# A graph attention layer: each node tile projected directly behind the transposes of its second block

## The chip, the core and the metric

The kernel runs on one core of a Trainium2 chip, in one launch. A core has five engines that work side by side, each through its own instructions in order: PE (TensorE, matrix products into PSUM), DVE (VectorE), ACT (ScalarE), POOL (GpSimd, which here issues the gathers) and SP (SyncE, which here issues loads and stores). They meet through semaphores. The metric is the device time of the whole launch in microseconds (us).

## The reference

The input x has 4096 rows of 512 values, all float32; adj is a 4096 x 4096 matrix in which under one entry in a hundred is above zero. Two layers follow each other, each on a layer norm with a relu, each added to x:

```python
# layer 0
h = relu(layernorm(x))
d = rowsum(adj) ** -0.5
x = x + relu((d[:, None] * adj * d[None, :]) @ h @ W0 + b0)
# layer 1
h = relu(layernorm(x))
hw = h @ W1
e = leaky_relu(hw @ a[:512] + (hw @ a[512:]).T, 0.2)      # 4096 x 4096
p = softmax(where(adj > 0,  e, -1e12), axis=1)
q = softmax(where(adj > 0, -e, -1e12), axis=1)
x = x + elu(concat([p @ h, -(q @ h)], axis=1) @ wtrans)   # wtrans: 1024 x 512
```

## The kernel before

Layer 0 is a dense product over adj, in groups of node tiles (a tile is 128 nodes). It also writes what layer 1 needs: for each node a row of a table in HBM (its h, its score, and its bits of the adjacency), and for each pair of blocks a list of the neighbours. Layer 1 uses that few entries of adj are above zero.

In layer 1 a **block** is 64 nodes, and a **pair** is two blocks, so one node tile. There are 32 pairs. The first of them (`PAIR0`, 16) is worked on at the end of layer 0, so that its transposed result `ut0` lies ready; the other 31 are worked on by `sparse_layer1`, whose list `order` holds their 62 blocks, two of a pair behind each other. Below, the even block of a pair is the first, the odd one the second.

For each pair GpSimd issues 22 indirect DMAs (`gather`, L487), each of which fetches 128 table rows of 644 words into SBUF. They go into three buffers: `g0` (8 gathers), `g1` (6) and `g2` (8). The even block of the pair uses `g0` and `g1`, the odd one `g1` and `g2`. Each of these buffers exists twice (`g_pools[k % 2, a]`), so that a pair shares its buffers with the pair two before it: a gather into one has to wait until that pair's last reader of it is done.

The work on one block r has these steps:

- `weights(r)`: for both of its buffers DVE adds the scores (z, L501), ACT and DVE make the leaky relu (L1633, L1634), ACT takes two exponentials (p, L513), for the two softmaxes, and DVE multiplies with the mask (L523). DVE then sums p (total, L1639).
- `product(r)`: PE sums total over the partitions (cs, L554), DVE makes the reciprocal (rl, L556 and L557); PE multiplies p with the gathered rows in 22 products (u, L530), and ACT scales the result into SBUF (us, L1667).
- `turn(r)`: PE transposes us in four parts (tp, L564), and ACT copies them into one half of the pair's tile `ut` in two copies (L569), one for each softmax.
- `finish1(n)`, once for a pair: SP loads the rows of x1 (L1677); PE multiplies `ut` with wtrans in eight products (o, L1681), four for each softmax; DVE and ACT make the elu and the addition (L1689 to L1693), and SP stores the tile (L1694).

The profile counts each float32 matmul as two, so a product of a block shows as 44 rows.

In `sparse_layer1` nobody writes the order of the engines by hand. The program is written down in the order of the loop over k (L1723 to L1744), and a scheduler builds each engine's order from it before the kernel runs; only some instructions (the gathers among them) are kept in program order. At step k the loop writes the product of block k, the gathers of a later pair, the weights of block k + 2, the transposes of block k - 1, and, at each odd k from 3 on, the projection of the pair that holds block k - 3. PAIR0 is projected at k = 2. Behind the loop come the last transposes and the last projection. Some other steps stand in the same loop: `copy_rows` (SP copies table rows to further tables), `load_s` (SP loads the score rows of coming blocks), and at k = 40 `judge`, a test whether the lists were long enough.

In the built program PE's order around one pair is, before the change: u of the even block; tp of the odd block of the pair before; u of the odd block; tp of the even block; o of the pair before; and so on with the next pair. ACT's order is: the exponentials of the next pair's even block; us of the even block; the two `ut` copies of the odd block of the pair before; the exponentials of the next pair's odd block; us of the odd block; the `ut` copies of the even block.

Of the kernel before, what the change touches and what calls it, by code (L numbers as in the profile page):

```python
# [269 lines left out]
def gcn_gat_kernel(  # L270
# [55 lines left out]
    def bank(name):  # L326
        return ps.tile([P, 512], F32, tag="ps", name=name)
# [4 lines left out]
    with sbuf(name="init", bufs=1) as init:  # L332
        column = init.tile([P, P], F32, name="column")
        nc.vector.memset(column[:, 0:1], 0.0)
        n = 1
# [140 lines left out]
    def copy_rows(queue, g, j, n):  # L476

        r = j // EJ * ER + j % EJ * P
        return queue.dma_start(
            out=table[g][r : r + n * P, :ROW_W], in_=table[tab0][r : r + n * P, :ROW_W]  # L480
        )
# [78 lines left out]
    def turn_u(r, u, ut):  # L560

        tp = ps.tile([P, FC, 2, 2, SB], F32, tag="ps", name=f"tp{r}")
        for c in range(FC):
            nc.tensor.transpose(  # L564
                tp[:, c].rearrange("p h g i -> p (h g i)"), u[:, c * P : (c + 1) * P], ident
            )
        for g in range(2):
            half = ut[:, g, :, (r % 2) * RB : (r % 2 + 1) * RB]
            nc.scalar.copy(half.rearrange("p c (h i) -> p c h i", h=2), tp[:, :, :, g, :])  # L569
# [4 lines left out]
    with sbuf(name="y0", bufs=1) as y_pool, sbuf(name="wa", bufs=1) as wa_pool, sbuf(name="bits", bufs=4) as bits_pool, sbuf(name="small0", bufs=4) as small, ExitStack() as rest, ExitStack() as lists:  # L574
# [473 lines left out]
        i0, n = GROUPS[0]  # L1048
        with sbuf(name="w0", bufs=1) as w0_pool, sbuf(name="ain", bufs=9) as ain, sbuf(name="xs", bufs=5) as x_pool, sbuf(name="at6", bufs=5) as at_pool, sbuf(name="bits6", bufs=3) as bits6, sbuf(name="ln", bufs=3) as ln_pool, sbuf(name="marks", bufs=6) as mark_pool:
# [32 lines left out]
            order = {engine.PE, engine.DVE, engine.Activation, engine.SP}  # L1082
            with tc.manual_schedule(engines=order):
# [37 lines left out]
                for j in range(NJ):  # L1121
                    q, turn = 4 * j + 5, j + 3 < NJ
# [443 lines left out]
    def sparse_layer1():  # L1566
        nonlocal verdict
        with ExitStack() as pools:
# [34 lines left out]
            gath, wgt, us, uts, srow = {}, {}, {}, {PAIR0: ut0}, {}  # L1603

            def load_s(k):

                srow[k] = s_pool.tile([P, 4 * P], F32, tag="s", name=f"s{k}")
                return nc.sync.dma_start(
                    out=srow[k], in_=s_dram[4 * k * P : 4 * (k + 1) * P].partition_broadcast(P)
                )  # L1610

            def gather1(n, a):
                k = pairs.index(n)
                gt = g_pools[k % 2, a].tile([P, CHUNKS[a], ROW], I32, tag="g", name=f"g{a}_{n}")
                gather(gt, n, a, True)
                gath.setdefault(n, []).append(gt)
# [6 lines left out]
            def weights(r):  # L1623

                nk = sum(CHUNKS[r % 2 : r % 2 + 2])
                p = p_pool.tile([P, nk, 2, 2, SB], F32, tag="p", name=f"p{r}")
                s = srow[r // 8][:, r % 8 * RB : (r % 8 + 1) * RB]

                for gt, k, n in parts(r):
                    z = bank(f"z{r}_{k}")[:, : n * RB].rearrange("p (k c) -> p k c", c=RB)  # L1630
                    scores(s, z, gt[:, :, ROW_T : ROW_T + 1].bitcast(F32))
                    y = tmp.tile([P, n, RB], F32, tag=f"y{n}", name=f"y{r}_{k}")
                    nc.scalar.activation(y, z, AF.Copy, scale=ALPHA)  # L1633
                    nc.vector.tensor_tensor(z, z, y, ALU.max)  # L1634
                    exps(z, p[:, k : k + n], leaky=False, pin=r in first)
                    mask_out(r, p[:, k : k + n], gt[:, :, ROW_W:].bitcast(U8))
                total = small.tile([P, 2 * RB], F32, tag="total", name=f"total{r}", bufs=3)
                q = p.rearrange("p k h g i -> p (h g i) k")
                nc.vector.tensor_reduce(total, q, AX.X, ALU.add)  # L1639
                for k in range(n_late if r in with_late else 0):  # L1640
                    q = lates[r][:, k].rearrange("p h g i -> p (h g i)")
                    nc.vector.tensor_tensor(total, total, q, ALU.add)
                wgt[r] = (p, total)
# [7 lines left out]
            def product(r):  # L1651
                p, total = wgt.pop(r)

                rl = None if r in first else inverse_sums(small, r, total)
                u = bank(f"u{r}")

                def row(k):
                    gt, k0, n = parts(r)[k >= parts(r)[1][1]]
                    return gt[:, k - k0, :F].bitcast(F32)

                half_products(r, u, p, row, HALVES[r % 2], r not in with_late)
                if r in with_late:
                    ks = range(n_late)
                    half_products(r, u, lates.pop(r), lambda k: late_h[:, k, :F], (ks, ks), begin=False)
                rl = rl or inverse_sums(small, r, total)
                us[r] = work.tile([P, F], F32, tag="us", name=f"us{r}")
                nc.scalar.activation(us[r], u, AF.Copy, scale=rl)  # L1667

            def turn(r):
                if r % 2 == 0:  # L1670
                    uts[r // 2] = ut_pool.tile([P, 2, FC, P], F32, tag="ut", name=f"ut{r // 2}")
                turn_u(r, us.pop(r), uts[r // 2])

            def finish1(j):
                ut = uts.pop(j)
                x1 = work.tile([P, F], F32, tag="x1", name=f"x1_{j}")
                nc.sync.dma_start(out=x1, in_=x1_dram[j])  # L1677
                po = bank(f"o1_{j}")
                for g in range(2):
                    for c in range(FC):  # L1680
                        nc.tensor.matmul(  # L1681
                            po,
                            ut[:, g, c, :],
                            wts[g][:, c, :],
                            start=g == 0 and c == 0,
                            stop=g == 1 and c == FC - 1,
                        )
                e = work.tile([P, F], F32, tag="eo", name=f"eo{j}", bufs=1)
                nc.vector.tensor_scalar(e, po, 0.0, None, ALU.min)  # L1689
                nc.scalar.activation(e, e, AF.Exp)  # L1690
                y = work.tile([P, F], F32, tag="y", name=f"y1_{j}", bufs=1)
                nc.vector.scalar_tensor_tensor(y, po, 0.0, x1, ALU.max, ALU.add)
                nc.vector.scalar_tensor_tensor(e, e, -1.0, y, ALU.add, ALU.add)  # L1693
                nc.sync.dma_start(out=out[j * P : (j + 1) * P, :], in_=e)  # L1694
# [7 lines left out]
            order = [r for n in pairs for r in (2 * n, 2 * n + 1)]  # L1702
# [20 lines left out]
            for k, r in enumerate(order):  # L1723
                product(r)
                if k % 6 == 1 and k // 6 < len(later):
                    for j, n in GROUPS[-2:]:
                        tc.keep_in_program_order(copy_rows(nc.sync, later[k // 6], j, n))
                if k + 4 - k % 2 < len(order):
                    for a in ((0,), (1, 2))[k % 2]:
                        gather1(order[k + 4 - k % 2] // 2, a)  # L1730
                if k + 2 < len(order):
                    weights(order[k + 2])
                    if wanted and order[k + 2] % 8 == 7:
                        load_s(wanted.pop(0))
                if k:
                    turn(order[k - 1])
                if k == 2:
                    finish1(PAIR0)
                if k == 40:
                    verdict = judge(small)  # L1740
                if k % 2 and k > 1:
                    finish1(order[k - 3] // 2)
            turn(order[-1])
            finish1(order[-1] // 2)  # L1744

    sparse_layer1()
    bad = nc.values_load(
        verdict[0:1, 0:1],
# [38 lines left out]
```

## Time and profile before

| what | us |
|---|---|
| median of 3 runs (lowest, highest) | 2099.77 (2090.87, 2101.19) |
| the profiled execution | 1951.6 |
| its span, first to last instruction | 1949.7 |
| granted TensorE clock, mean share of full speed | 0.984 |
| start of the products of `sparse_layer1` | 1053.7 |
| first issue of the last gather | 1899.0 |
| o of the last tile starts | 1934.2 |

The profile shows one execution. For each engine it gives when it was busy; a matmul's end is modelled, so PE's busy time is an upper reading. A row of an instruction group is: source line, engine, operation, what it writes and reads (buffer numbers left out), count, then busy time in us with the mean of one in ns, and the time that the engine sat idle just before, with what ended that. A row of the timeline is: start, duration, engine, line, operation and, in brackets, the idle time before it and what released it. A row of the waits is: who waited for what, us in total, times, and the longest. In the rows of DMA issues the last number is the median time in us from issue to landing.

The same stage in windows of time (from the span's start; busy time of each engine, with the number of instructions, the granted clock, the share of time that the DMA engines were busy, and GB/s):

```profile
1200.00:1400.00 200.00, 199.61 (x852) 76.59 (x849) 123.63 (x177) 61.48 (x133) 153.09 (x155) 1.00 0.89 292
1400.00:1600.00 200.00, 191.69 (x802) 73.72 (x800) 122.18 (x174) 60.85 (x132) 153.39 (x154) 0.99 0.89 289
1600.00:1800.00 200.00, 192.68 (x816) 73.94 (x814) 122.88 (x176) 60.90 (x133) 153.17 (x154) 1.00 0.87 274
```

The five busy columns are PE's matmuls, PE's weight loads, DVE, ACT and POOL.

### The profile page before, as it was taken

The page shows a single profiled execution, that of the slowest core. Times are in us where ns is not written, and L with a number is a line of the kernel's source. Part 1 is how long each engine was busy: PE and PEld are TensorE (multiplying, and loading weights), DVE is VectorE, ACT ScalarE, POOL GpSimd, SP SyncE. Part 2 cuts the span into 40 slices and gives each one's busy share as a digit, 9 for nine tenths or more (in the row PEclk, how much of TensorE's full clock was granted, in tenths as well). Part 3 has the DMA queues.
Part 4 walks back from the last instruction along what each step waited for, and adds up shares of the span by engine and source line. Part 5 has one row for each costly group of instructions (what it writes and reads, how often), then busy time and mean ns, then how long its engine had stood idle before and what let it go on. Part 6 is the DMA issues. An engine that isn't in the chain of part 4 may idle for free.

```text
span 1949.7 us, 23088 instructions
## 1 busy us (share of the span) xinstructions
PE 1858.9 (95%) x7752; PEld 1038.0 (53%) x7752; DVE 1317.1 (68%) x2879; ACT 636.2 (33%) x1185; POOL 902.6 (46%) x978
## 2 busy tenths in 40 slices
PE   7999989999999999999597999999999999999998
PEld 3444438888888888888332333333333333333333
DVE  5666659747897999896446766566566656656653
ACT  5777752112122212121122333233233223323321
POOL 2101001001232322232367777777777777777770
PEclk9999999999999999999798999999999999999999
DMA  9999955778467575867579898989889888888880
GB/s 350 371 336 335 332 199 193 241 223 282 132 198 238 170 256 169 265 208 235 156 242 345 259 316 278 311 270 312 291 292 301 274 281 265 282 277 261 275 277 31
DMA packets 185206, 503.47 MB, mean 258 GB/s; under 512 B 29107, under 2 KB 37971, under 8 KB 185078
## 3 DMA queue, kind: packets, MB, share of 16 engines
q0 software_dynamic: 70128, 265.46, 42.4%
q1 hardware_dynamic: 108832, 225.80, 34.1%
q10 hardware_dynamic: 6118, 10.64, 1.5%
q8 instruction: 63, 1.03, 0.2%
q14 instruction: 65, 0.53, 0.1%
HBM read 457.44 MB, written 103.02 MB: 287 GB/s over the span
## 4 chain that ended last, share of the span: by engine, by line
PE 63%; POOL 11%; DMA 10%; issue 9%; DVE 5%; ACT 1%; SPq 0%; DVEq 0%; POOLq 0%; ACTq 0%
PE p L1020 24%; PE u L530 15%; POOL g L487 11%; PE o L1681 7%; PE yp L809 6%; PE acc L979 5%; DMA g<-table,idx 4%; DMA ld<-li,off 3%; PE q L1354 2%; DMA at<-in_adj_t 1%; PE tp L564 1%; PE counts L794 1%; PE tx L758 1%; DVE p L523 1%; DMA xt<-in_x 1%
## 5 line engine op out<-in xcount | busy, mean ns | idle before, releaser
L487 POOL DMA_INDIRECT g<-table,idx x704 | 702.9, 998 | 224.4 <-issue 197.7
L530 PE MATMUL u<-g,p 128*64 128x512 f32 x2728 | 600.5, 596 | 4.2 <-DVE p L523 4.2
L530 PEld LDWEIGHTS u<-g,p 128*64 128x64 f32 x2728 | 190.8, 137 | 361.4 <-issue 333.2
L501 DVE TENSOR_TENSOR z<-g,s 128x512 f32<-128x512 f32 (+1 forms) x124 | 78.2, 631 | 283.2 <-DMA g<-table,idx 232.7
L1020 PE MATMUL p<-y,at 128*128 128x256 f32 x832 | 249.8, 382 | 5.7 <-DVE w L893 4.8
L1020 PE MATMUL p<-t,sums 128*128 128x256 f32 x832 | 246.4, 381 | 7.3 <-DVE t L994 7.3
L1020 PE MATMUL p<-y,sums 128*128 128x256 f32 x832 | 248.6, 380 | 0.0
L849 ACT ACTIVATE m<-at 128x1024 uint8<-128x1024 f32 x110 | 116.1, 1056 | 405.7 <-DMA at<-in_adj_t 356.1
L434 POOL DMA_INDIRECT ld<-li,off x112 | 101.8, 909 | 315.8 <-DMA ld<-li,off 271.7
L1633 ACT ACTIVATE y<-z 128x512 f32<-128x512 f32 (+1 forms) x124 | 67.4, 544 | 523.1 <-DVE z L501 417.2
L1681 PE MATMUL o<-wt,ut 128*128 128x512 f32 x512 | 226.1, 595 | 0.5 <-ACT ut L569 0.5
L1639 DVE TENSOR_REDUCE total<-p 128x128 f32<-128x1792 f32 x62 | 201.8, 3255 | 2.1
L1020 PEld LDWEIGHTS p<-t,sums 128*128 128x128 f32 x832 | 158.4, 191 | 29.3 <-DVE t L994 7.8
L1020 PEld LDWEIGHTS p<-y,at 128*128 128x128 f32 x832 | 157.6, 191 | 30.5 <-DVE w L893 5.6
L1020 PEld LDWEIGHTS p<-y,sums 128*128 128x128 f32 x832 | 159.0, 191 | 21.9
L859 POOL DMA_DIRECT2D table<-m x63 | 51.0, 810 | 245.0 <-ACT m L849 152.1
L523 DVE SCALAR_TENSOR_TENSOR p<-g,p 128x512 f32<-128x512 uint8 (+1 forms) x248 | 141.1, 620 | 20.9 <-ACT p L513 20.9
L1681 PEld LDWEIGHTS o<-wt,ut 128*128 128x128 f32 x512 | 95.3, 191 | 108.4 <-issue 106.7
L513 ACT ACTIVATE p<-z 128x512 f32<-128x512 f32 (+1 forms) x248 | 119.8, 542 | 54.8 <-DVE z L1634 54.8
L779 ACT ACTIVATE junk<-ar 128x1024 bf16<-128x1024 f32 x128 | 134.5, 1051 | 4.3 <-issue 2.1
L1020 PE MATMUL p<-t,at 128*128 128x256 f32 x416 | 124.9, 382 | 0.0
L979 PE MATMUL acc<-y,at 128*128 128x512 f32 x256 | 120.2, 594 | 0.0
(207 smaller groups left out, 1892.8 us busy)
## 6 DMA issues: line engine op xcount, KB each, us to landing
ar<-in_adj SPq DMA_DIRECT2D x128, 512.0 KB, 5.7
at<-in_adj_t SPq DMA_DIRECT2D x112, 512.0 KB, 5.1
table<-table SPq DMA_DIRECT2D x49, 1032.0 KB, 9.0
table<-m POOLq DMA_DIRECT2D x55, 256.0 KB, 4.9
g<-table,idx POOLq DMA_INDIRECT x704, 4.4
at<-in_adj_t SPq DMA_DIRECT2D x32, 256.0 KB, 6.1
xr<-in_x SPq DMA_DIRECT2D x32, 256.0 KB, 6.9
x<-x1d SPq DMA_DIRECT2D x32, 256.0 KB, 5.4
```

Of the source, the lines that this page charges most:

```text
L434: return nc.gpsimd.indirect_dma_start(out=lst_dram[g][:, :], out_offset=bass.IndirectOffsetOnAxis(ap=off[g][:, e, c : c + 1], axis=0), in_ ...
L487: i = nc.gpsimd.indirect_dma_start(out=gt[:, k, :], out_offset=None, in_=table[2 * n // RPT], in_offset=bass.IndirectOffsetOnAxis(ap=idx[n ...
L513: i = nc.scalar.activation(p[:, :, :, g], z, AF.Exp, scale=(1.0, -1.0)[g])
L523: nc.vector.scalar_tensor_tensor(e, m, 0.0, e, ALU.is_gt, ALU.mult)
L530: i = nc.tensor.matmul(u[h * RB : (h + 1) * RB], p[:, k, h].rearrange("p g i -> p (g i)"), row(k), start=begin and k == HALVES[r % 2][h][0 ...
L779: nc.scalar.activation(junk, ar, AF.Identity, accum_out=parts[j][:, c : c + 1])
L809: nc.tensor.matmul(yp, hx_t[j][:, c * P : (c + 1) * P], w0_sb[:, c, :], start=c == 0, stop=c == FC - 1,)
L849: nc.scalar.activation(m, at, AF.Sign)
L979: nc.tensor.matmul(a, at[:, 0, it * P : (it + 1) * P], y0[j], start=j == 0, stop=j == NJ - 1)
L1020: i = nc.tensor.matmul(out, left[:, x * P : (x + 1) * P], right, start=jp == 0 and first, stop=jp == NP - 1 and (final or not first),)
L1639: nc.vector.tensor_reduce(total, q, AX.X, ALU.add)
L1681: nc.tensor.matmul(po, ut[:, g, c, :], wts[g][:, c, :], start=g == 0 and c == 0, stop=g == 1 and c == FC - 1,)
```

## The change

Only the loop of `sparse_layer1` is changed. The transposes of a block still come one step after its product, and the projection of a pair now comes in the same step as the transposes of its odd block (at even k, directly behind `turn`), where before it came one step later. PAIR0 is projected at k = 1 instead of 2. For the last three blocks the transposes come in the same step as the block's own product, and the last two pairs are projected in the step of their odd block.

```diff
-                if k:
+                if k and order[k - 1] in us:
                     turn(order[k - 1])
-                if k == 2:
+                if k == 1:
                     finish1(PAIR0)
                 if k == 40:
                     verdict = judge(small)
-                if k % 2 and k > 1:
-                    finish1(order[k - 3] // 2)
-            turn(order[-1])
-            finish1(order[-1] // 2)
+                if k + 4 > len(order):
+                    turn(order[k])
+                if k % 2 == 0 and k:
+                    n = order[k - 1] // 2
+                    if n in uts:
+                        finish1(n)
+                if k % 2 and order[k] not in us:
+                    finish1(order[k] // 2)
```

`us` and `uts` are dictionaries of what waits to be transposed and to be projected. Number, shape and operands of the instructions stay what they were; the order on the engines changes.

In the built program PE's order around one pair becomes: u of the even block; tp of the odd block of the pair before; o of the pair before; u of the odd block; tp of the even block. ACT's order of exponentials, us and `ut` copies stays; ACT's exponential of the elu and DVE's three instructions of it come one block earlier. On DVE the mask of the first half of an even block comes ahead of the score addition of its second half, where before it came behind it. At the end PE's order is: u of the odd block of the last but one pair, tp of both its blocks, o of that pair, u and tp of the even block of the last pair, u and tp of its odd block, o.

## The prediction

> **What bounds the kernel now.** I read the page's first part, then the gather's group and what GpSimd waits for, then PE's waits in layer 1, then the last pair in order of time.
>
> ```profile
> PE 1858.9 (95%) x7752; PEld 1038.0 (53%) x7752; DVE 1317.1 (68%) x2879; ACT 636.2 (33%) x1185; POOL 902.6 (46%) x978
> ...
> L487 POOL DMA_INDIRECT g<-table,idx x704 | 702.9, 998 | 224.4 <-issue 197.7
> ...
> g<-table,idx POOLq DMA_INDIRECT x704, 4.4
> ```
>
> ```profile
> POOL g L487 <- issue: 187.3, 615, 0.3
> POOL g L487 <- DMA g<-table,idx: 4.6, 15, 0.3
> ...
> PE tp L564 <- ACT us L1667: 20.3, 17, 3.6
> ```
>
> PE is 95% busy, but a share of the span says nothing of one stage. From 1030 us on, GpSimd issues the 22 gathers of each pair with never more than the 0.3 us between two of them that it always has (last number of each wait row): no gather waits for a buffer. The first gathers of pairs 2 and 31 (numbered in gathered order, pair 0 made early) start at 1039.9 and 1871.65, 29 pairs apart: 28.68 us a pair. PE's own work is shorter: a pair is two products, two transposes and a projection,
>
> ```profile
> 1882.34 0.94 POOL L487 DMA_INDIRECT g<-table,idx  x1 [0.30 <-issue]
> ...
> 1894.54 0.57 DVE L501 TENSOR_TENSOR z<-g,s 128x384 f32<-128x384 f32 x1 [6.03 <-DMA g<-table,idx]
> ...
> 1897.58 0.69 ACT L1667 ACTIVATE us<-u,rl 128x512 f32<-128x512 f32 x1
> 1898.14 0.66 ACT L569 COPY ut<-tp 128x256 f32<-128x256 f32 x2
> ...
> 1898.32 0.65 PE L564 MATMUL tp<-ident,us 128*128 128x128 f32 x4 [1.10 <-ACT us L1667]
> ...
> 1898.81 7.03 PE L1681 MATMUL o<-wt,ut 128*128 128x512 f32 x16
> ...
> 1905.89 9.66 PE L530 MATMUL u<-g,p 128*64 128x512 f32 x44
> ...
> 1925.78 0.65 PE L564 MATMUL tp<-ident,us 128*128 128x128 f32 x4
> 1925.94 0.69 ACT L1667 ACTIVATE us<-u,rl 128x512 f32<-128x512 f32 x1 [9.07 <-PE u L530]
> ...
> 1926.53 0.64 ACT L569 COPY ut<-tp 128x256 f32<-128x256 f32 x2
> ```
>
> that is o to u 7.08, u 9.59, tp with cs 0.71, u 9.59, tp 0.49 (differences of starts): 27.46 us. PE therefore catches up with the gathers and then waits about 1 us a pair for us of the even block. The reader is to see why us is late: it was free to run once its product ended (1897.1), but ACT works in order, and before it stand the exponentials of the even block of the next pair, which need that pair's middle buffer (the second of three, six gathers, first issue 1882.34). So **the gather issue sets the pace of layer 1**; the end is paced by the last buffers and then by PE alone.
>
> **The change, part by part.**
>
> *Projection one product earlier (29 pairs).* In the built program PE's order per pair becomes u(even), tp(odd before), o, u(odd), tp(even); before, u(odd) and tp(even) stood between tp(odd before) and o. Counts and shapes of every instruction are the same. The new wait: o needs the ACT copies of the transpose just ahead of it. On ACT these copies stand behind us(even) and behind the next pair's even exponentials, both before and after. Queued behind the waiting o on PE are cs, u(odd), tp(even) and u of the next pair; who waits for u(odd) is GpSimd, since its 12th of 22 products is the last reader of the middle buffer that the pair after next is gathered into. That gives three loops from one projection to the next.
>
> 1. Gather issue: 28.68 us, as now.
> 2. PE: 7.08 + 9.59 + 0.71 + 9.59, then from the start of tp until o: us starts 0.16 later, the first copy 0.59 after that, takes 0.36 (o's first four products read only that half), and 0.05 to PE: 1.16. Sum 28.13, 0.67 more than now. The nearest row is the last tile of today, where o follows its transposes at once: the wait is 0.46 us there, without an us in between.
>
> ```profile
> 1933.14 0.60 PE L564 MATMUL tp<-ident,us 128*128 128x128 f32 x4
> ...
> 1934.20 7.13 PE L1681 MATMUL o<-wt,ut 128*128 128x512 f32 x16 [0.46 <-ACT ut L569]
> ```
>
> 3. Buffer: o to u(odd) 7.08, 12 of 22 products 5.24, release about 0.1, first middle gather to us(even) 15.24 (1882.34 to 1897.58), us to o 0.97 (0.56 + 0.36 + 0.05). Sum 28.63. Over the last pairs the 15.24 varies up to 15.6. Against that, DVE's new order puts the mask of the first half (two instructions, 1.2 us) ahead of the add at 1894.54 instead of behind it, off this path: about 0.5 less, so 28.1 to 29.0. Today this loop has some 12 us to spare, because u(odd) is done before us(even) is asked for.
>
> All three come out within half a microsecond of each other, and GpSimd's is the longest or nearly so. So the 20.3 us of waiting at tp moves to o and is not added to. What is added: at the start PE is still close behind the buffers (the second pair's o must wait for 4 exponentials queued on ACT; the fourth pair's middle buffer is then asked for 1 to 3 us before it is free), and pairs whose issue was quick can't be made up. Carrying the three loops forward pair by pair with the trace's own gather times moves the last middle gather by 2.4 us with the 0.5 gained and 7.8 us without it. I take 5.
>
> [...]
>
> *Clock.* [...]
>
> ```profile
> 1412.26 1.12 PE L564 MATMUL tp<-ident,us 128*128 128x128 f32 x4 [3.56 <-ACT us L1667]
> 1413.17 8.01 PE L1681 MATMUL o<-wt,ut 128*128 128x512 f32 x16
> ```
>
> There tp took 1.12 instead of 0.66 and o 8.01 instead of 7.03: 1.4 us lost after one gap. Gaps of 0.8 to 1.7 us lost nothing after them (0.66 again). The new gaps are of that second kind, so I add nothing[...].
>
> *What moves with o.* Per tile three DVE instructions, one ACT exponential, one load of x1 and one store on SP. DVE comes to the first of them when o ends, 7.1 after o's start; then the odd weights (to 18.4) and the first half of the next even ones (to 22.7) follow by their durations, and the next middle buffer's add is due at about 25: 2.4 us to spare; without it each us late adds to loop 3. On SP the store passes the next load and, at three places, a pair of table copies and one load of s; SP idles most of the stage, the s rows are needed pairs later: nothing. If s came late, DVE's add would wait for one landing, some 5 us, a few times.
>
> *The first projection* (pair 0) goes two turns earlier, its input is long done: nothing.
>
> *The last three blocks.* From the start of the third last projection (1898.81) to the end (1949.7) it is 50.9 us now, with two products behind it. Afterwards three are behind it, as the odd one of the last but one pair was done before that point and now comes after: o and u 16.67, wait for us (0.16 + 0.69 + 0.05) 0.9, tp and copies 1.1, o 7.07, u 9.6, wait 0.9, tp and cs 0.7, u 9.6, wait 0.9, tp and copy 1.06, o until DVE 7.17, DVE and store 8.33 (1941.37 to 1949.7): 64.0, so +13. Projecting the last but one tile earlier saves nothing: PE has the same work.
>
> **Sum:** 5 + 13 = 18 us on the profiled execution's 1951.6 (span 1949.7): 1970. The median of the runs shown, 2099.77, is 148 us above that execution, and the profile can't say why. If the runs have a slower PE, loop 2 decides throughout: 29 x 0.67 + about 3 at the end = 22. Between both, **+20: 2120 us.**
>
> **Rivals.**
>
> *A, the buffer loop decides.* If the landing is 1 us longer than in this profile (its rows go from 3.8 to 7.4), loop 3 is at 29.7, 1.0 over the issue on 28 pairs: 18 + 28 = 46, 2146 us; for each further us 28 more. For: DMA is 87 to 89% busy in this stage. Against: a held-up gather thins out the DMAs, and the 0.5 of DVE's new order.
>
> *B, hidden.* The early shift stays away and waits overlap; the end alone costs something, about 6 if the last gathers come a little earlier in PE's order: 2106, no change that can be measured.
>
> *C, faster.* The 20.3 us of waits at tp vanish, since us gains a projection's 7 us, and o's new wait is short while ACT is two thirds idle: 2079. It decides if GpSimd can issue faster than now; all 615 of its gaps being the same 0.3 speaks against it, and so does the end.
>
> *D, it doesn't do what it says:* excluded by the built program's order.
>
> **Chances.** Forecast 0.60 (own range 2109 to 2132), A 0.18, B 0.16, C 0.06. A measurement of this kernel can't tell less than about 0.5%, 10.5 us. Faster is C: 0.06; no change is B and the forecast's lowest edge: 0.18; slower the rest: 0.76. Range 2104 to 2155: half of B, C and A's worst stay out.
>
> **What would show it.** Right: GpSimd's gaps stay at 0.3 us nearly everywhere, the tp wait is replaced by about 1 us at o behind ut in nearly every pair, PE busy unchanged, and some 64 us from the third last projection to the end. Gaps at the middle buffer's first gather in many pairs mean A. Gathers of a pair in clearly under 28.6 us, or a shorter end, would make me wrong.

## The result: 2476 us instead of 2100

| | median, us | lowest to highest | runs |
|---|---|---|---|
| before | 2100.48 | 2090.87 to 2103.06 | 4 |
| after | 2476.01 | 2445.85 to 2484.64 | 4 |

The ratio is 1.175, with a 95% interval from 1.164 to 1.186: slower, by 376 us where the prediction said 20. Executions of these kernels fall into two groups, whatever the chip (chip 5 showed both), and those taken side by side fell into the same one: before takes 1951 to 1959 us in **the 1955 group** and 2084 to 2107 us in **the 2100 group**. The profile shown ahead of the change is of the 1955 group; the times of the table above, and the profile after, are of the 2100 group.

The page of after (2484.64 us, span 2482.8), with the groups that answer to those shown of before:

```profile
PE 1952.2 (79%) x7752; PEld 1071.2 (43%) x7752; DVE 1325.2 (53%) x2879; ACT 646.6 (26%) x1185; POOL 894.2 (36%) x978
...
L487 POOL DMA_INDIRECT g<-table,idx x704 | 696.0, 989 | 738.5 <-DVE z L1634 451.5
L1681 PE MATMUL o<-wt,ut 128*128 128x512 f32 x512 | 301.7, 755 | 437.0 <-ACT ut L569 330.3
...
g<-table,idx POOLq DMA_INDIRECT x704
```

The projection in the profile before:

```profile
L1681 PE MATMUL o<-wt,ut 128*128 128x512 f32 x512 | 226.1, 595 | 0.5 <-ACT ut L569 0.5
```

It had 0.5 us of idle time ahead of it in all and now has 437, and its own busy time went from 226.1 to 301.7. GpSimd idles 738 us instead of 224. The last line of the page of after lacks its time to landing: the trace holds too few semaphore events to work one out, which matters below. The waits of layer 1 (1100 to 2430 us; who waited for what, us in total, times, longest):

```profile
POOL g L487 <- DVE z L1634: 451.5, 31, 20.0
ACT us L1667 <- remote: 352.3, 27, 17.8
...
PE o L1681 <- ACT ut L569: 329.3, 20, 17.5
```

By the timeline of POOL the first gather into a middle buffer now waits in 30 of the 32 gathered pairs, 8 to 21 us. To see what for, one pair in order of time:

```profile
1333.32 0.94 POOL L487 DMA_INDIRECT g<-table,idx  x1 [19.24 <-DVE z L1634]
...
1337.96 9.66 PE L530 MATMUL u<-g,p 128*64 128x512 f32 x44
...
1346.23 0.87 ACT L513 ACTIVATE p<-z 128x384 f32<-128x384 f32 x2 [0.63 <-issue]
...
1347.56 0.66 PE L564 MATMUL tp<-ident,us 128*128 128x128 f32 x4
...
1360.35 0.94 POOL L487 DMA_INDIRECT g<-table,idx  x1 [0.30 <-issue]
1364.73 0.69 ACT L1667 ACTIVATE us<-u,rl 128x512 f32<-128x512 f32 x1 [17.62 <-remote]
1365.31 0.64 ACT L569 COPY ut<-tp 128x256 f32<-128x256 f32 x2
...
1365.73 4.64 PE L1681 MATMUL o<-wt,ut 128*128 128x512 f32 x5 [17.51 <-ACT ut L569]
...
1380.83 0.94 POOL L487 DMA_INDIRECT g<-table,idx  x1 [19.54 <-DVE z L1634]
```

The first row is the first gather into a middle buffer. From there the exponentials are through at 1347.1, 13.8 us later, so us could start within the 15.24 of the prediction. PE's row of u (the even block's product) ends at 1347.6 and nothing else stands ahead of us on ACT; yet us starts 17.1 us later, and PE idles from 1348.2 to 1365.7. The only semaphore that us waits for is PE's, raised by the last product of u, and the trace has that rise at 1364.70. The profile cannot say who raised it ("remote"), because by its rows PE had been done for long. Here the two ends of a matmul must be told apart, that of its row and its signal. A row of u lasts 597 ns in the mean by the page, though the rows follow each other at 0.22 us (9.66 for 44): rows overlap. In this pair the end of the last row (1347.6) and the signal (1364.70) are 17.1 us apart, and us starts 0.03 us behind the signal. **PE's signal is late, not ACT.**

The rows show one thing more. The gather at 1360.35 is the last that GpSimd issues before it waits for its next middle buffer; o starts 5.4 us later, and the next gather into a middle buffer at 1380.83, once PE has got through o and 12 products behind it. In 18 of 28 pairs o starts 4.6 to 5.4 us after such a last gather. There GpSimd and PE take turns instead of working side by side.

### The profile page after: what moved, and what is told of

The parts are those of the page before. It is cut to its first block, busy times and chain, and to the rows that moved or that the text cites. A ratio compares the mean times of both kernels' runs of the same rounds, so it can differ in the third digit from the quotient of the medians.

```text
span 2482.8 us, 23023 instructions
## 1 busy us (share of the span) xinstructions
PE 1952.2 (79%) x7752; PEld 1071.2 (43%) x7752; DVE 1325.2 (53%) x2879; ACT 646.6 (26%) x1185; POOL 894.2 (36%) x978
## 4 chain that ended last, share of the span: by engine, by line
PE 48%; another core or an unknown queue 15%; issue 11%; DVE 10%; DMA 7%; ACT 4%; POOL 3%; SPq 0%; DVEq 0%; POOLq 0%; ACTq 0%
PE p L1020 19%; PE o L1681 12%; PE u L530 5%; PE yp L809 5%; PE acc L979 4%; DMA g<-table,idx 3%; POOL g L487 3%; DMA ld<-li,off 2%; DVE z L501 1%; DMA at<-in_adj_t 1%; PE q L1354 1%; ACT p L513 1%; ACT y L1633 1%; DVE z L1634 1%
## 5 line engine op out<-in xcount | busy, mean ns | idle before, releaser
L1681 PE MATMUL o<-wt,ut 128*128 128x512 f32 x512 | 301.7, 755 | 437.0 <-ACT ut L569 330.3
L530 PE MATMUL u<-g,p 128*64 128x512 f32 x2728 | 607.2, 597 | 10.2 <-issue 6.0
L1681 PEld LDWEIGHTS o<-wt,ut 128*128 128x128 f32 x512 | 122.5, 247 | 597.8 <-ACT ut L569 335.4
L1689 DVE TENSOR_SCALAR eo<-o 128x512 f32<-128x512 f32 x32 | 22.1, 692 | 630.2 <-PE o L1681 625.7
L434 POOL DMA_INDIRECT ld<-li,off x112 | 100.6, 898 | 306.9 <-DMA ld<-li,off 268.9
L1667 ACT ACTIVATE us<-u,rl 128x512 f32<-128x512 f32 x62 | 42.6, 687 | 469.0 <-remote 352.3
L859 POOL DMA_DIRECT2D table<-m x63 | 50.9, 808 | 253.0 <-ACT m L849 157.9
```

The source lines that it names most:

```text
L434: return nc.gpsimd.indirect_dma_start(out=lst_dram[g][:, :], out_offset=bass.IndirectOffsetOnAxis(ap=off[g][:, e, c : c + 1], axis=0), in_ ...
L530: i = nc.tensor.matmul(u[h * RB : (h + 1) * RB], p[:, k, h].rearrange("p g i -> p (g i)"), row(k), start=begin and k == HALVES[r % 2][h][0 ...
L1681: nc.tensor.matmul(po, ut[:, g, c, :], wts[g][:, c, :], start=g == 0 and c == 0, stop=g == 1 and c == FC - 1,)
```

## The experiments

Means of a pair are taken from the start of the second projection to that of the third last, over 28, from each run's trace. Each experiment that fell into the 2100 group is one execution. Code is shown in part.

### The kernel before, in the 2100 group

> The kernel before, unaltered, for its profile. Where the runs beside it take 1955: a profile like the first one, within 10 us of 1951.6. Where they take 2100: if PE's finished products are signalled late there as in the profile after, the waits that us and the ut copies have behind PE grow to some us, but half of the lateness lies beside the next block's product; PE's row of u or tp shows idle time of about 5 us a pair (148 us over 29 pairs). Rival: the gathers are slower there, and GpSimd's gaps or the landings grow instead.

It took 2099.7 us, beside 2107.05 for before. A pair took 32.3 us there, against 28.3 in the 1955 group. The waits of us behind PE (1100 to 2040 us), as expected:

```profile
ACT us L1667 <- remote: 106.9, 10, 16.8
ACT us L1667 <- PE cs L554: 105.0, 15, 14.1
ACT us L1667 <- PE tp L564: 80.2, 12, 7.5
ACT us L1667 <- PE u L530: 71.4, 16, 16.6
```

They are 364 us together, where the profile of before in the 1955 group has 1.7 (1100 to 1900 us). Lateness itself can be counted in the traces, from the end of u's row to the start of a us that waited, over the last 58 blocks (29 pairs). It is at most 0.1 us a block in before and after_again (the changed kernel in the 1955 group, below). In before_again it is up to 17.1 us and 170 in all; in after up to 17.1 us and 358 in all, 356 of it at even blocks. So before meets late signals as well, but about half as much of them. PE's rows of before_again (start, duration):

```profile
1869.33 0.59 PE L530 MATMUL u<-g,p 128*64 128x512 f32 x1 [0.64 <-issue]
1870.74 0.59 PE L530 MATMUL u<-g,p 128*64 128x512 f32 x1 [0.82 <-issue]
1871.45 0.27 PE L564 MATMUL tp<-ident,us 128*128 128x128 f32 x1
1872.17 0.54 PE L564 MATMUL tp<-ident,us 128*128 128x128 f32 x3 [0.45 <-issue]
```

Products that start 0.22 us apart in the mean elsewhere (9.66 us for 44) are 1.41 or 0.71 us apart for a few instructions, and PE waits for nothing that the profile shows. The same in after at the start of layer 1, first PE's products, then its weight loads:

```profile
1093.46 1.01 PE L530 MATMUL u<-g,p 128*64 128x512 f32 x1 [1.09 <-issue]
1094.88 1.01 PE L530 MATMUL u<-g,p 128*64 128x512 f32 x1 [0.42 <-issue]
1096.30 1.01 PE L530 MATMUL u<-g,p 128*64 128x512 f32 x1 [0.40 <-issue]
```

```profile
1094.16 0.18 PEld L530 LDWEIGHTS u<-g,p 128*64 128x64 f32 x1 [1.22 <-issue]
1095.59 0.18 PEld L530 LDWEIGHTS u<-g,p 128*64 128x64 f32 x1 [1.24 <-issue]
```

Load, product, load, product: one instruction each 0.7 us. In after's long waits the rows of u and tp look prompt, but their signals reach ACT anything from 0.06 us (the pair shown above) to 5.6 us apart, instead of 0.6. Whether PE works late there or only signals late, the rows can't say. The expected 5 us of idle rows a pair did not come out as such (PE's idle time from 1100 to 2040 us sums to 78 us); the rest is in products that took longer (PE's busy time rose from 1858.9 to 1934.0) and in late signals.

### Is it the change, the group, or both

> The changed kernel once more, unaltered. The loop alone took 33 us more and the end alone 13 us more than a before of 1955 us. If loop and end add up, 1955 + 33 + 13 = 2001 us where before takes 1955, and the 2476 belongs to executions in which before takes 2100. If loop and end together make what neither makes alone, 2400 or more beside a before of 1955.

In the 1955 group: 1991.47 us beside 1957.53, ratio 1.018 (1.016 to 1.021). So the change costs 34 us there and 376 in the 2100 group. All of the wait at o (us in total, times, longest, 1060 to 1930 us):

```profile
PE o L1681 <- ACT ut L569: 32.9, 29, 4.8
```

| execution | span, us | a pair, us | third last projection to end, us |
|---|---|---|---|
| before, 1955 group (first profile) | 1949.7 | 28.30 | 50.9 |
| after_again, 1955 group | 1987.7 | 29.19 | 64.3 |
| before_again, 2100 group | 2097.9 | 32.30 | 51.0 |
| after, 2100 group | 2482.8 | 45.81 | 67.3 |

The 2100 group adds 4.0 us a pair to before and 16.6 to after; 28 times the difference of 45.81 and 32.30 is 378 of the 385 us between the two spans.

### Does lateness alone do it

The `ut` copies of an odd block's transposes are made eight times over, in both kernels and in 27 pairs (`more` is set for these):

```diff
-        for g in range(2):
+        for g in [0, 1] * (8 if more else 1):
```

> The kernel before, with the ut copies of an odd block's transposes made eight times over (14 further copies of about 0.3 us on ACT, 4.2 us, in 27 to 29 pairs), so that the projection's input is late by that much. Turnaround theory (before, one block's product of 9.6 us lies between transposes and projection and hides any lateness; after the change nothing does): within 6 us of before, the lateness shows once. Rival (ACT's 4.2 us a pair are a cost in themselves, or delay us and the buffers): 60 us or more over before.

> The changed kernel with the same 14 further copies a pair. Turnaround theory: each pair waits 4.2 us longer at o, and as the gap then passes some 2.2 us the projection runs partly at half clock, 1.7 us more: 5.9 x 28 = 165 us over the 1991 of the changed kernel, 2155. Rival (PE has slack to take it up, since the gathers set the pace): under 2030.

Both ran in the 1955 group, beside 1955.51. e6_late_before: **1955.41**, nothing. e7_late_after: **2127.41**, 136 over the 1991 of the changed kernel. PE's rows from the odd block's transposes to the projection, first of e6, then of e7:

```profile
1692.11 0.66 PE L564 MATMUL tp<-ident,us 128*128 128x128 f32 x4
...
1692.81 9.66 PE L530 MATMUL u<-g,p 128*64 128x512 f32 x44
1702.40 0.66 PE L564 MATMUL tp<-ident,us 128*128 128x128 f32 x4
1703.97 7.13 PE L1681 MATMUL o<-wt,ut 128*128 128x512 f32 x16 [0.91 <-ACT ut L569]
```

```profile
1678.88 0.66 PE L564 MATMUL tp<-ident,us 128*128 128x128 f32 x4
1683.87 9.45 PE L1681 MATMUL o<-wt,ut 128*128 128x512 f32 x16 [4.33 <-ACT ut L569]
```

In before, a whole product lies between the odd block's transposes and o, and takes the 4 us up but for waits like the 0.91. After the change o waits 4.33 instead of 0.46, and runs 9.45 (8.83 in other pairs) instead of 7.13; the granted clock (the 0.50) is half from within the gap on:

```profile
1681.70:1688.50 6.80, 4.63 (x6) 2.05 (x7) 1.12 (x2) 2.79 (x10) 5.28 (x6) 0.50 0.82 262
```

A pair is 34.1 instead of 28.2: 5.9, as expected. Over the 29.19 that after_again takes in the mean, disturbed pairs included (next section), it is 5.0, so the sum stays under the 165. This is the multiplier: **4 us of lateness between PE's transposes and the projection's input are paid in each pair after the change, where before pays nothing**.

### Which part, and what costs 34 us in the 1955 group

e1_loop undoes the new end (shown, against after); e2_tail keeps the loop of before and has the new end alone (not shown):

```diff
-                if k + 4 > len(order):
-                    turn(order[k])
                 if k % 2 == 0 and k:
-                    n = order[k - 1] // 2
-                    if n in uts:
-                        finish1(n)
-                if k % 2 and order[k] not in us:
-                    finish1(order[k] // 2)
+                    finish1(order[k - 1] // 2)
+            turn(order[-1])
+            finish1(order[-1] // 2)
```

> The projections of the loop come one product earlier, as in the change, but the last three blocks are done in the order of before. Buffer theory (a pair's turn from the first middle gather through exponentials, us, transposes and projection back to the release of the middle buffer sets the pace, and it is 46 to 48 us long in the profile after): the loop alone costs nearly all, 2465 us (2476 less the 13 that I gave the end). Rival (the new end costs most, or end and loop only together): under 2200.

> The loop of before with the new order of the last three blocks alone. Buffer theory: 13 us more than before, by the sum of the prediction, so a ratio of 1.006. Rival (the end is where the time is lost): over 2200 us.

Both ran in the 1955 group, beside 1955.12. e1_loop 1988.07 (ratio 1.017, 1.014 to 1.019), e2_tail 1968.28 (1.007, 1.005 to 1.009). The 2465 expected of the loop was a number of the other group, so nothing can be read from it; the 13 of the end is met. The parts don't add: once the loop moves an odd block's product behind the third last projection, the end is as long with the old order (62.7 us in e1_loop) as with the new (64.3). The same two once more, with what each group would show:

> As e1_loop, the loop's projections earlier, the end as before. Where the before beside it takes 2100: if the serial turn of transposes, copies and projection in the loop is what multiplies PE's lateness, 2430 to 2475, all of the loss but the 13 us of the end; rival (the new end is where it breaks): under 2200. Where it takes 1955: 1988 again.

> As e2_tail, the loop of before with the new order of the last three blocks. Where the before beside it takes 2100: 2105 to 2125, since no gathers are left to slow PE when the last three blocks are worked on; rival (the end is hit as well): over 2140. Where it takes 1955: 1968 again.

Both fell in the 1955 group (1993.53 beside 1957.89, 1971.49 beside 1956.60). Which part costs the 376 there is thus read from the table above alone: the pairs.

In after_again a pair takes 28.19 us where nothing disturbs it:

```profile
1344.43 0.66 PE L564 MATMUL tp<-ident,us 128*128 128x128 f32 x4
1345.55 7.13 PE L1681 MATMUL o<-wt,ut 128*128 128x512 f32 x16 [0.46 <-ACT ut L569]
```

That is loop 2 of the prediction (28.13). Over it, 28 us are lost: 10.6 in the first three pairs, and 16.3 in four later ones like this:

```profile
1284.63 0.66 PE L564 MATMUL tp<-ident,us 128*128 128x128 f32 x4
1287.48 8.83 PE L1681 MATMUL o<-wt,ut 128*128 128x512 f32 x16 [2.20 <-ACT ut L569]
```

They come every third pair, where SP copies table rows; the last gather ahead of the middle buffer lands after 7.2 to 7.6 us there. In e8_split the two copies are taken apart:

```diff
-                if k % 6 == 1 and k // 6 < len(later):
-                    for j, n in GROUPS[-2:]:
-                        tc.keep_in_program_order(copy_rows(nc.sync, later[k // 6], j, n))
+                if k % 6 in (1, 4) and k // 6 < len(later):
+                    j, n = GROUPS[-2 + (k % 6 == 4)]
+                    tc.keep_in_program_order(copy_rows(nc.sync, later[k // 6], j, n))
```

> The changed kernel with the two table copies of SP that come together in every third pair taken apart by one and a half pairs. In the profile of after_again the last gathers ahead of the middle buffer land after 7.2 to 7.6 us instead of about 5 in four such pairs, o then waits 2.2 to 3.5 us, runs 8.83 instead of 7.13 us, and the four pairs lose 16 us together. If the copies make these landings late, most of the four gaps fall under 2 us: 8 to 16 us less than 1991, 1975 to 1983. If they are not the cause: 1991 within 4.

1978.72 us, ratio to before 1.011 (1.008 to 1.014): 23 us over before instead of 34. The time came out as forecast, the gaps only in part: two of the four fell under 2 us (1.55 and 0.67), two remain (3.03 and 2.33), and a new one of 2.23 came up. A pair takes 29.07 us in the mean instead of 29.19, which is 3.4 of the 8.4 us between the two spans; 4.9 lie ahead of the second projection, which the copies don't explain. The copies have a part in the late pairs, but how large it is stays open.

### Does PE need the gathers to be late

From the fifth gathered pair on the gathers are left out:

```diff
-                gt = g_pools[k % 2, a].tile([P, CHUNKS[a], ROW], I32, tag="g", name=f"g{a}_{n}")
-                gather(gt, n, a, True)
+                if k < 4:
+                    gt = g_pools[k % 2, a].tile([P, CHUNKS[a], ROW], I32, tag="g", name=f"g{a}_{n}")
+                    gather(gt, n, a, True)
+                else:
+                    gt = gath[pairs[k - 2]][a]
```

> The changed kernel without the gathers from the fifth gathered pair on: those pairs work on the rows that lie in the buffers already; all other instructions and PE's order stay. In the profile after, us of the even block starts 17 us after the last product that it reads has ended by its row. Theory S (PE's work or its signals come late while gathers are moving): no such gap is left, PE's loop of 28.1 us a pair or the 27.5 of its work sets the pace, about 1900 to 1930 us at the before run's 2100 scale. Theory B (PE holds back the signal of a finished product while the instruction right behind, the projection's, waits for ACT): the gap of up to 17 us stays in most pairs, over 2300 us.

> As e3_no_gathers. Where the before beside it takes 1955: 1974 again. Where it takes 2100, theory S (PE's work or its signals come late while gathers are moving): still within 30 us of 1974, with no gap of 10 us or more between the end of u and us. Rival (PE itself is slower there, gathers or not): above 2100.

> As e3_no_gathers. Where the before beside it takes 2100: theory S (PE's work or its signals come late while gathers are moving) says that the lateness is left only in the first four pairs, so 1970 to 2030; the rival (PE is slower in such an execution, gathers or not) says above 2100. Where it takes 1955: 1970 again, and nothing is learnt.

The first two fell in the 1955 group (1974.07 and 1967.84), where the question doesn't arise. The third met the 2100 group: **1996.04** beside 2103.52. The changed kernel without gathers is 107 us faster there than before with them, and all pairs from the fourth on take the undisturbed 28.19. The same stretch in several kernels (windows: us, busy us and instructions of PE, PE's loads, DVE, ACT, POOL, then granted clock, DMA share, GB/s), after first, then no_gathers_3:

```profile
1400.00:1600.00 200.00, 120.82 (x464) 46.16 (x464) 71.71 (x100) 37.44 (x78) 93.34 (x96) 0.78 0.58 180
```

```profile
1400.00:1600.00 200.00, 196.75 (x823) 75.37 (x823) 124.39 (x177) 62.08 (x134) 0.00 (x0) 1.00 0.12 36
```

Is it the bytes? In e5_plain and plain_2 SP brings as many:

```diff
-                gather(gt, n, a, True)
+                if k < 4:
+                    gather(gt, n, a, True)
+                else:
+                    for c in range(CHUNKS[a]):
+                        rows = table[2 * n // RPT][c * P : (c + 1) * P, :]
+                        tc.keep_in_program_order(nc.sync.dma_start(out=gt[:, c, :], in_=rows))
```

> From the fifth gathered pair on each gather is replaced by a plain DMA of SP that brings 128 rows of the same table, one after the other, into the same place (same bytes, other rows, so other results). Where before takes 2100: if GpSimd's issuing makes PE's signals late, the gap between u and us is gone and the time 2000 to 2100; if the moving bytes make them late, gaps of 10 us or more stay and the time is over 2300. Where before takes 1955: SP issues faster than GpSimd, so PE's loop of 28.2 us a pair decides: 1960 to 2000.

> As e5_plain: SP brings the same number of bytes with plain transfers from the fifth gathered pair on, GpSimd issues nothing. Where the before beside it takes 2100: if moving bytes make PE late, most pairs take 40 to 48 us, over 2300 us; if GpSimd's gathers do, 1970 to 2030. Where it takes 1955: 1973 again.

SP issues faster than GpSimd, as the expectation says: in the profile of before its loads and stores take 0.32 to 0.34 us each to issue (1200 to 1400 us), the gathers 998 ns in the mean. 1972.8 in the 1955 group. In the 2100 group **1999.93** beside 2095.59, at 300 GB/s, where the gathers of before moved 289 in the same window in the 1955 group and 260 in the 2100 group; plain_2:

```profile
1400.00:1600.00 200.00, 196.03 (x818) 75.05 (x817) 125.74 (x176) 64.41 (x134) 0.00 (x0) 1.00 0.84 300
```

Last, the same with `nc.gpsimd.dma_start`, so that GpSimd issues them:

> As e5_plain, but the plain transfers of 128 table rows are issued by GpSimd instead of SP, in the place of its gathers from the fifth gathered pair on. Where the before beside it takes 2100: if any issue by GpSimd makes PE late, over 2200 us; if it is the indirect gather alone, 1970 to 2030. Where it takes 1955: 1960 to 2000.

**1999.28** beside 2084.27, and the window shows GpSimd at work:

```profile
1400.00:1600.00 200.00, 196.75 (x820) 75.36 (x819) 127.09 (x177) 64.68 (x134) 83.52 (x156) 1.00 0.82 301
```

So neither the bytes nor every issue by GpSimd makes PE late: the indirect gathers do. What it is about them stays open: the plain transfers read rows one after the other, and the order of the rows was not tried by itself.

### Is it the waiting instruction behind

Theory B of the expectations says that PE holds a signal back while the instruction right behind it waits. Two products more, which wait for nothing else, go in after the transposes of an odd block:

```diff
+                if r % 2 and r not in order[-4:]:
+                    more = bank(f"more{r}")
+                    for c in range(2):
+                        nc.tensor.matmul(more, u[:, c * P : (c + 1) * P], wts[0][:, c, :], start=c == 0, stop=c == 1)
```

> The changed kernel with two more products on PE (1.76 us by the rows of o) between the transposes of the odd block and the projection that waits for them; they wait for nothing else. Theory B: the signals of u and tp no longer have a waiting instruction right behind them and arrive at once; the pair falls to about 30 us, so 2180 us or less. Theory S: the gap between the end of u by its row and us stays at 10 to 17 us, and the time at 2440 to 2530.

> As e4_more, two products more ahead of each waiting projection. Where the before beside it takes 1955: 1997 again. Where it takes 2100: theory B (a signal is held back while the instruction right behind it waits) says 2200 or less; theory S says 2440 or more.

> As e4_more: two products more, which wait for nothing else, between the transposes and the waiting projection. Where the before beside it takes 2100: theory B (a signal is held back while the instruction right behind it waits) says 2200 or less; theory G (PE's own pace falls while GpSimd gathers, whatever stands behind) says within 60 us of the 2476 of the changed kernel, rather above it. Where it takes 1955: 1997 again.

1997.49 and 1996.45 in the 1955 group, 6 us over after_again for 51 us more of PE work. In the 2100 group 2289.81 beside 2084.27: a pair takes 39.1 us, between what the two theories said (30 and 46). Both are wrong as put. What stands behind the transposes does matter, as 186 us less for more work show, but waits at o of up to 15.6 us remain. Why is open.

## Why the prediction was wrong

- **What bounds, and the three loops.** Two sums hold in the 1955 group: PE's loop 28.19 (28.13 said), the third last projection to the end 64.3 (64.0 said). The wait at o is 0.46 in most pairs, as on the last tile of before. Which loop decides does not hold even there: an undisturbed pair takes the same 28.19 as in no_gathers_3, where nothing is gathered, so PE sets the pace and not the issue of the gathers, which was said to need 28.68.
- **The early shift of 5 us.** Mis-sized: 28 pairs took 25 us more than before in after_again (29.19 against 28.30). The three loops were carried on with landings as they were in before, where late ones were hidden; four came after 7.2 to 7.6 us next to the table copies, and o waited.
- **The clock, "I add nothing".** Wrong. The prediction had one gap of 3.56 us with a loss behind it and gaps of 0.8 to 1.7 us without, and took the new ones for the second kind. Over the profiles of the 1955 group no gap of up to 1.55 us ahead of o cost anything, every one from 2.59 us on made o 8.6 to 10 us long instead of 7.13, and between them 7 of 18 did; one of 1.62 us was enough. These two items are what is missing in the 1955 group: 38 us between the spans of after_again and of the first profile, where the sum said 18; 34 between the medians, where the forecast said 20. In the 2100 group the gaps are long ones: in after 29 of them, 3.55 to 17.54 us, stand ahead of an o of 8.5 to 10.2 us, and the granted clock is 0.50 from 1353.3 to 1370.3, around the o shown above, and 1.00 from there to 1397.6. The 76 us by which o's busy time rose (226.1 to 301.7) are a fifth of the 376; the 1.4 us lost behind the one gap of 3.56, in 28 pairs, would be 39.
- **The step that failed** is in the sum: the runs were 148 us above the profiled execution, and I wrote that if "the runs have a slower PE, loop 2 decides throughout: 29 x 0.67 + about 3 at the end = 22". That took a slower PE as slower products, which cost each order alike, and priced the new wait at 0.67. What the runs have is PE completing, or signalling, late while GpSimd gathers. In before PE has a product to do meanwhile: us is late by 5.9 us a pair (170 over 29), and a pair grows by 32.30 - 28.30 = 4.0. After the change u, us, the copies and o are one serial turn with no other work of PE in it: us is late by 12.3 us a pair (358 over 29), and a pair grows by 16.6, o's half clock (0.50) included. Why the lateness itself doubles is not shown. The next middle buffer is released only behind that o, so GpSimd stops too. The wait priced at 0.67 measured up to 17.5. The difference of 148 us was the warning, and it was read as a scale.
- **Rival A** has the right place, gaps at the middle buffer's first gather in 30 pairs, and the right loop, but 13.5 us a pair (45.81 - 32.30) where it had 1.0, and the wrong cause: not the landings but PE's signal to us. B and C fell in both groups. What makes PE late is not in the prediction at all, and stays open.

## What to carry to other kernels

An instruction that waits for another engine's answer to the one just ahead of it can turn a late signal into idle time as often as the loop runs; keep one block of independent work in between, even if the wait looks like half a microsecond in a good profile (0.46 us in after_again, up to 17.5 in after). Before pricing a new wait, delay its input on purpose in both orders: here 4 us of repeated copies cost 0 in one and 136 us in the other, in a run each. Where the runs lie 7% off the profiled execution, find out what differs before forecasting on either of them.

## What was unexpected

In the 2100 group PE's rows stand 0.7 us apart in stretches, or its signals come late, from about the first gather of layer 1 on and no longer once the gathers are left out or replaced. Layer 0 takes the same time in both groups (the first of these gathers starts at 978.3 in after, at 980.4 in after_again), although GpSimd issues 112 other indirect DMAs there (L434, 898 ns each in the mean); so it is not every indirect DMA. The trace itself thins out in the same place: some 1500 semaphore events per 100 us in the 1955 group, 325 to 450 in the 2100 group, back to 1500 in plain_2 as soon as its gathers end. PE's lateness and the missing records come together; whether one brings the other or a third thing brings both, no run here shows, and what puts an execution in one group or the other was not found. No run here compares executions with and without the recording of the trace either, so whether part of the 376 us belongs to it stays open.
